# Last block's LayerNorm scales issued ahead of the ssm sums, its turns two products sooner, its sums in another order, one Square a product later

## The chip, the cores and the metric

The kernel runs on one core of a Trainium2 chip. Its engines are TensorE (PE in the profile; PEld is its weight load), VectorE (DVE), ScalarE (ACT), GpSimd (POOL) and SyncE (SP), which here only issues DMAs. The metric is the device time of one execution in microseconds (us). Before the change the median of three runs is 588.91 us (588.4 to 589.07).

## The reference

One transformer-like block on `x` of 2 x 2048 tokens by 512, with a condition vector per sequence, all in float32:

```python
emb = jnp.dot(silu(t), ada_w) + ada_b          # six rows of 512: shift, scale, gate for each half
norm = _ln(x) * (1.0 + scale_msa) + shift_msa
h = gelu(jnp.dot(norm, ssm_w1) + ssm_b1)       # exact gelu, 512 -> 512
x = x + gate_msa * (jnp.dot(h, ssm_w2) + ssm_b2)
norm2 = _ln(x) * (1.0 + scale_mlp) + shift_mlp
hf = gelu_tanh(jnp.dot(norm2, ff_w1) + ff_b1)  # 512 -> 1024
x = x + gate_mlp * (jnp.dot(hf, ff_w2) + ff_b2)
```

`_ln` takes mean and variance over the 512 features with eps 1e-6.

## The kernel before

**Tiles and blocks.** The 4096 tokens are cut into 8 blocks of 512, numbered 0 to 7. A block's `x` is a tile of 128 partitions by 4 rows by 512 features. Every matrix product is done by Strassen-Winograd schemes: seven products P1 to P7 of half-size operands in place of eight, with operands that are sums of quarters. The sums of the moving or the stationary operand are made by GpSimd or VectorE (`cut_sum`, line 348). The big ff product goes further, with 26 products (table `HK_P`) of registers that are sums of sixteenths (GpSimd, line 923, program `HK_B`).

**Stages.** For block i there are four products on TensorE: hA_i (first ssm product, line 475), oA_i (second, with the residual, line 475), hC_i (first ff product, 26 products in line 985, method `Second.products`), oC_i (second ff product, lines 778 and 824). For block 5, which the change speaks of, TensorE does in order hC_5, oA_6, hA_7, oC_5.

**LayerNorm.** Class `Norm`; n1[i] is the norm ahead of ssm, n2[i] the one ahead of ff. Its steps: statistics (`stats`, VectorE, lines 512 and 513; or on ScalarE, `sums_on_act`, line 524, and `squares_on_act`, line 535, with one tiny GpSimd operation `less`, line 540); `scales`, eight tiny GpSimd operations (lines 548 to 566) for 1/std and -mean/std; `normal(c)` for each of the four rows c on ScalarE (line 580); `turn(c)`, a 32 x 32 block transpose on VectorE (line 591) into the tile `blocks`; `move`, 16 DMAs of 64 KB issued by SP (line 600) that finish the transposition; `moved`, four ScalarE operations with scale and shift of the condition (line 623); `summed`, four sums for the Winograd operands (line 348). For n1[7] the four sums are made by VectorE into a tile `nS`: nS0 = q12 - q11, nS1 = q22 - nS0, q12 in place = q22 - q12 (`x<-x` in the profile), nS2 = q21 - nS1.

**Order.** Nothing is scheduled by a tool: each engine runs its instructions in the order in which the program issues them. `group` and `products` issue a product's matmuls, then what reads its PSUM bank (`after`), then the operations that were hooked to this product with `hook(hooks, places, ops)`, one place for each operation, the last place for all that are left. In `products` the places are the numbers 0 to 25. In a residual with the order `CARRIED` the products run as P1, P5, P6, P2, P7, P3, P4, but the places keep the names P1, P2, P6, P5, P7, P3, P4 by position: the place named P6 comes after the third product, P5 after the fourth, P7 after the fifth.

**PSUM.** In `products` there are six banks, two tiles for each of y, x and v. A bank is read by ScalarE for a destination's first term (line 999) or by VectorE for a further one (line 1002), and the next product into that bank waits for the reading; gelu is line 980. In a residual, P6, P7 and P4 (and P1) share bank y; VectorE reads a product into `x` in line 739, and P4 waits for the reading of P7.

**Where blocks differ.** In the loop from line 1278, `ahead` is true for i = 5 alone: there n1[7] is prepared in hC_5, and hA_7 follows oA_6 before oC_5. `unread_stats` is filled for i = 4 alone: the Squares of n1[6] are done by ScalarE inside hC_4 (line 1293).

Of the kernel before, what the change touches and what calls it, by code (L numbers as in the profile page):

```python
# [140 lines left out]
def kernel(  # L141
# [16 lines left out]
    nc = tc.nc  # L158
# [40 lines left out]
    def load_x(i, pieces=1):  # L199
        xs[i] = big_tile(f"x_{i}")  # L200
        for s in range(pieces):
            c = slice(s * C // pieces, (s + 1) * C // pieces)
            nc.sync.dma_start(out=xs[i][:, c, :], in_=x_blk[i][:, c, :])
# [209 lines left out]
    def leaves_of_weight(w_sb, s, engs):  # L413


        def views(w):
            v = w.rearrange("p (h k) (q e d) -> p h k q e d", h=2, e=2, d=P)
            return {f"{h + 1}{e + 1}": v[:, h, :, :, e, :] for h in range(2) for e in range(2)}

        lo, hi = w_sb[:, : w_sb.shape[1] // 2, :], w_sb[:, w_sb.shape[1] // 2 :, :]  # L420
        q23, t23 = views(hi), thirds(pair_t)
        o23 = second_operands(q23, t23)
        ops = {p: {n: v[:, :, j, :] for n, v in o23.items()} for j, p in enumerate(("P2", "P3"))}
        sums = {"P23": sums_of_second(q23, t23, engs["P23"])}
        for j, (p, w) in enumerate((("P4", s[:, 2]), ("P5", s[:, 0]), ("P7", lo[:, :, D // 2 :]))):
            q, t = {n: v[:, :, 0, :] for n, v in views(w).items()}, thirds(fw2_t[:, 2 + j])
            ops[p] = second_operands(q, t)
            sums[p] = sums_of_second(q, t, engs[p])
        return ops, sums
# [8 lines left out]
    def seed(name, row, part, leaf=False):  # L438


        b, cols = (("y", row[:, : D // 2]), ("v", row[:, D // 2 :]))[part]
        t = ps_g.tile([P, 2, HT], F32, tag=b, name=f"p{b}_{name}_{len(seeds.get((name, b), ()))}")
        seeds.setdefault((name, b), []).append(t)
        if part == 1 and leaf:
            nc.scalar.copy(t[:, 0, :P], cols[:, :P])
        else:
            nc.scalar.copy(t, cols.unsqueeze(1).to_broadcast([P, 2, HT]))
# [45 lines left out]
    def hook(hooks, places, ops):  # L493

        for n, op in enumerate(ops):
            hooks.setdefault(places[min(n, len(places) - 1)], []).append(op)
# [226 lines left out]
    def residual(name, i, hops, wops, kdim, hooks, last=False, order=ORDER):  # L723

        xt = xs[i]
        F = D // 2
        q = {
            "11": xt[:, 0:2, :F],
            "12": xt[:, 0:2, F:],
            "21": xt[:, 2:4, :F],  # L730
            "22": xt[:, 2:4, F:],
        }
        dest = {"P1": "11", "P2": "11", "P6": "12", "P5": "22", "P7": "22", "P3": "12", "P4": "21"}

        def after(p, ps, js):
            if p == "P1" and order is CARRIED:
                return
            d = q[dest[p]][:, js]
            nc.vector.tensor_tensor(d, ps[BANK[p]][:, js], d, ALU.add)  # L739
            if last and p in ("P7", "P4"):  # L740
                s = slice(2 + js.start, 2 + js.stop)
                f = slice(F, D) if p == "P7" else slice(0, F)
                nc.sync.dma_start(out=out_blk[i][:, s, f], in_=xt[:, s, f])

        parted = ("P1", "P6", "P7", "P4") if last else ()
        places = ORDER if order is CARRIED else None
        group(name, kdim, hops, lambda p, j, k: wops[p][:, k, :], after, hooks, parted, order, places)
# [306 lines left out]
    def run(ops):  # L1054
        for op in ops:
            op()
# [4 lines left out]
    n1 = {0: Norm(0, 1), 1: Norm(1, 1)}  # L1061
# [70 lines left out]
    gb, hA = {2: b2_bc}, {}  # L1132
# [12 lines left out]
    hooks = {}  # L1145
# [12 lines left out]
    hooks = {}  # L1158
# [26 lines left out]
    hooks = {}  # L1185
# [19 lines left out]
    hooks = {}  # L1205
# [14 lines left out]
    hooks = {}  # L1220
# [25 lines left out]
    hooks = {}  # L1246
# [10 lines left out]
    hooks = {}  # L1257
# [7 lines left out]
    hooks = {}  # L1265
# [11 lines left out]
    later, unread_stats = [], []  # L1277
    for i in range(1, NBLK):
        five = True
        nxt, nx2, last = i + 1 < NBLK, i + 2 < NBLK, i + 1 == NBLK  # L1280
        ahead, alone = i + 3 == NBLK, not nx2
        hC = Second(i)
        hooks = {}
        if i == 1:
            hook(hooks, range(0, 26), take(len(fa_sums)))
        if i == 1:
            engs = {"P23": nc.gpsimd, "P4": nc.gpsimd, "P5": nc.vector, "P7": nc.vector}
            leaf_wops, ops = leaves_of_weight(fw2_sb, fw2_s, engs)
            hook(hooks, (5, 7, 9, 11, 13, 14, 15, 16), ops["P23"] + ops["P4"])
            later = ops["P5"] + ops["P7"]  # L1290
            hook(hooks, (0,), [n1[i + 2].scales])
        elif unread_stats:
            hook(hooks, (1, 1, 3, 5, 7), unread_stats)
        if nx2:
            hook(hooks, (3,), [lambda: load_x(i + 1)])
            hook(hooks, (1, 2, 3, 4), hA[i + 1].summed(nc.gpsimd))
        elif nxt:
            hook(hooks, (1, 3), last_stats[2:])
            hook(hooks, (3,), [n2[i + 1].scales])
            hook(hooks, (15, 17, 19, 21), [lambda c=c: n2[i + 1].normal(c) for c in range(C)])  # L1300
            hook(hooks, (17, 19, 21, 23), [lambda c=c: n2[i + 1].turn(c) for c in range(C)])
            hook(hooks, (23,), [n2[i + 1].move])
        if nx2 and i > 1:
            hook(hooks, (7,) if unread_stats else (5,), [n1[i + 2].scales])
        if nx2:
            hook(hooks, (20, 24), [lambda p=p: seed(f"oA_{i + 1}", gb[2], p) for p in range(2)])
        else:
            hook(hooks, (20, 24), [lambda p=p: seed(f"oC_{i}", gb[5], p, five) for p in range(2)])
        if nx2:
            at = (12, 14, 16, 18) if i == 1 else (9, 11, 13, 15) if ahead else (15, 17, 19, 21)  # L1310
            hook(hooks, at, [lambda c=c: n1[i + 2].normal(c) for c in range(C)])
            hook(hooks, [n + 2 for n in at], [lambda c=c: n1[i + 2].turn(c) for c in range(C)])
            hook(hooks, (at[-1] + 2,), [n1[i + 2].move])
# [13 lines left out]
        hooks = {}  # L1327
# [12 lines left out]
        if nx2:  # L1340

            hook(hooks, ("P1",) if ahead else ("P7",), n1[i + 2].moved())
            if ahead:
                hook(hooks, ("P6", "P5", "P7"), n1[i + 2].summed(nc.vector, True))
            if i == 1:
                hook(hooks, ("P1", "P1", "P2", "P6"), later[:4])
            if fold:
                hook(hooks, ("P1", "P2", "P6", "P5"), fold[5:6] + fold[4:5] + later[:2])
            oC_seeds = [lambda p=p: seed(f"oC_{i}", gb[5], p, five) for p in range(2)]
            if not ahead:  # L1350
                hook(hooks, ("P2", "P6"), oC_seeds)
            n2[i + 1] = Norm(i + 1, 2)
            hook(hooks, ("P3", "P4"), n2[i + 1].stats())
            residual(f"oA_{i + 1}", i + 1, hA[i + 1], w2_ops, KD // 2, hooks, order=CARRIED)
            if ahead:
                hooks = {}
                hook(hooks, ("P2", "P6"), oC_seeds)
                hA[i + 2] = First(i + 2, n1[i + 2].ops, hooks, CARRIED, on_act=("P6", "P5"))
        else:
            for p in EARLY:  # L1360
                run(hooks.get(p, ()))
        leaf_fold, fold = (fold or i == 1) and later[2 if fold else 4 :], None

        hooks = {}
# [63 lines left out]
        hooks = {}  # L1428
# [7 lines left out]
        if i + 3 < NBLK:  # L1436
            st = n1[i + 3].sums_on_act() if refold5 else n1[i + 3].stats()
            unread_stats = n1[i + 3].squares_on_act() if refold5 else []
# [53 lines left out]
```

## Time and profile before

| | |
|---|---|
| median of three runs | 588.91 us (588.4 to 589.07) |
| the profiled execution | 589.1 us, span 587.3 us |
| granted TensorE clock | 0.999 |
| busy PE, PEld | 99%, 88% of the span |
| busy DVE, ACT, POOL | 71%, 45%, 73% |
| HBM read, written | 32.80 MB, 8.40 MB |

A line of a timeline has the start in us from the start of the span, the duration in us (of a merged group, from its first start to its last end), engine, line of the kernel, operation, written tile <- read tiles, partitions x elements, how many were merged, and in brackets how long the engine had been idle before it and what ended that. A line of waits has the waiting instruction, what it waited for, the total in us, how many times, and the longest. A line L348 or L923 is that of a helper; the tiles tell which step it is. hClo and hChi are the output of hC, hSC its sums, hSA the sums of hA.

### The profile page before, as it was taken

How to read it: one execution, taken by the hardware profiler on the slowest of the kernel's cores; microseconds unless marked ns; L12 is line 12 of the kernel's file. 1: busy time of each engine (PE TensorE's matmuls, PEld its weight loads, DVE VectorE, ACT ScalarE, POOL GpSimd, SP SyncE). 2: the span in 40 equal slices, each digit the busy share in tenths (PEclk: the TensorE clock that was granted, in tenths of full speed). 3: DMA queues.
4: the chain of work that ended last, by engine and by line, in shares of the span. 5: the costliest groups of instructions: out<-in, count | busy, mean ns of one | idle time of the engine just before them, and what ended most of it. 6: DMA issues, size and time to landing. Idle time of an engine off the chain costs nothing.

```text
span 587.3 us, 9483 instructions
## 1 busy us (share of the span) xinstructions
PE 579.2 (99%) x3303; PEld 516.4 (88%) x3303; DVE 415.9 (71%) x752; ACT 263.2 (45%) x479; POOL 428.4 (73%) x518
## 2 busy tenths in 40 slices
PE   8999999999999999999999999999999999999997
PEld 5888888888899888998889988998887998899896
DVE  4978888997867375676756858783747366787677
ACT  2234357405642554435732588235564431732420
POOL 1875359999997938969698899988587545369351
PEclk9999999999999999999999999999999999999999
DMA  8990322303206303361033711153030330031002
GB/s 316 395 392 9 91 68 81 104 37 107 59 15 187 119 1 81 111 203 71 6 87 83 276 73 31 42 140 145 4 73 0 104 113 1 1 73 71 2 1 71
DMA packets 25243, 56.49 MB, mean 96 GB/s; under 512 B 4672, under 2 KB 5740, under 8 KB 23532
## 3 DMA queue, kind: packets, MB, share of 16 engines
q1 hardware_dynamic: 21856, 51.67, 27.6%
q10 hardware_dynamic: 3340, 4.22, 2.9%
q8 instruction: 26, 0.43, 0.3%
q14 instruction: 21, 0.17, 0.1%
HBM read 32.80 MB, written 8.40 MB: 70 GB/s over the span
## 4 chain that ended last, share of the span: by engine, by line
PE 73%; POOL 11%; DVE 5%; DMA 5%; issue 3%; SPq 1%; ACT 1%; POOLq 0%; DVEq 0%
PE py_oA L475 7%; PE px_hC L985 7%; PE py_oC L778 7%; PE py_hA L475 7%; PE pl_oC_P_y L824 6%; PE py_hC L985 6%; PE pv_hC L985 6%; PE pl_oC_P_v L824 4%; PE pv_oA L475 4%; PE pv_hA L475 3%; PE py_oC L475 2%; PE py_hC L475 2%; DMA ada<-in_L_cond_ada_w_dram 2%; PE pl_oC_P_x L824 2%; POOL forms L923 2%
## 5 line engine op out<-in xcount | busy, mean ns | idle before, releaser
L348 POOL TENSOR_TENSOR hSC<-hClo,hChi 128x512 f32<-128x512 f32 (+1 forms) x16 | 19.2, 1205 | 40.8 <-ACT hChi L980 36.0
L623 ACT ACTIVATE nT<-nT,mod,mod 128x512 f32<-128x512 f32 x32 | 23.4, 802 | 55.6 <-DMA nT<-blocks 40.1
L512 DVE BATCH_NORM_STATS2 st<-x 128x6 f32<-128x512 f32 x60 | 40.7, 678 | 5.3 <-DMA x<-in_x_dram 5.0
L923 POOL TENSOR_TENSOR forms<-forms 128x256 f32<-128x256 f32 x56 | 41.8, 746 | 3.3
L985 PE MATMUL py_hC<-forms,fw 128*128 128x256 f32 x168 | 41.0, 380 | 0.1
L1002 DVE TENSOR_TENSOR hClo<-hClo,py_hC 128x512 f32<-128x512 f32 x42 | 28.6, 685 | 15.4 <-ACT hClo L999 9.4
L985 PEld LDWEIGHTS py_hC<-forms,fw 128*128 128x128 f32 x168 | 31.7, 190 | 4.9 <-DVE hClo L1002 0.5
L623 ACT ACTIVATE x<-x,mod,mod 128x512 f32<-128x512 f32 x24 | 17.6, 802 | 33.8 <-DMA x<-blocks 33.8
L591 DVE STREAM_TRANSPOSE blocks<-nT 128x512 f32<-128x512 f32 x32 | 22.2, 705 | 13.8 <-ACT nT L580 13.8
L923 POOL TENSOR_TENSOR forms<-nT,forms 128x256 f32<-128x256 f32 x42 | 30.6, 748 | 1.7 <-PE pl_oC_P_v L824 1.3
L1002 DVE TENSOR_TENSOR hChi<-hChi,pv_hC 128x512 f32<-128x512 f32 x35 | 23.3, 681 | 10.4 <-PE pv_hC L985 5.5
L923 POOL TENSOR_TENSOR forms<-nT 128x256 f32<-128x256 f32 x14 | 10.4, 740 | 27.6 <-ACT nT L623 20.7
L580 ACT ACTIVATE nT<-x,nmr,rstd 128x512 f32<-128x512 f32 x32 | 24.1, 806 | 13.2 <-POOL nmr L566 13.2
L985 PE MATMUL px_hC<-forms,fw 128*128 128x256 f32 x112 | 27.7, 380 | 0.5 <-ACT hClo L999 0.5
L980 ACT ACTIVATE hClo<-hClo,colsT 128x256 f32<-128x256 f32 x56 | 25.2, 498 | 4.2 <-DVE hClo L1002 4.0
L838 DVE TENSOR_TENSOR x<-pl_oC_P_y,x 128x256 f32<-128x256 f32 (+1 forms) x66 | 24.7, 375 | 3.1 <-PE pl_oC_P_y L824 1.5
L475 PE MATMUL py_oA<-w,hA 128*128 128x256 f32 x112 | 26.5, 379 | 0.0
L980 ACT ACTIVATE hChi<-hChi,colsT 128x256 f32<-128x256 f32 x56 | 25.1, 496 | 2.0 <-DVE hChi L1002 1.9
L739 DVE TENSOR_TENSOR x<-py_oA,x 128x512 f32<-128x512 f32 x26 | 17.9, 687 | 11.4 <-PE py_oA L475 10.8
L999 ACT ACTIVATE hChi<-py_hC 128x512 f32<-128x512 f32 x14 | 7.6, 593 | 40.9 <-POOL forms L923 21.0
L778 PE MATMUL py_oC<-fw_s,hSC 128*128 128x256 f32 x112 | 25.3, 380 | 0.0
L778 PE MATMUL py_oC<-fw,hClo 128*128 128x256 f32 x112 | 25.3, 379 | 0.0
(339 smaller groups left out, 1782.7 us busy)
## 6 DMA issues: line engine op xcount, KB each, us to landing
x<-in_x_dram SPq DMA_DIRECT2D x13, 1024.0 KB
out_dram<-x SPq DMA_DIRECT2D x14, 512.0 KB
ada<-in_L_cond_ada_w_dram SPq DMA_DIRECT2D x6, 1024.0 KB
x<-blocks SPq DMA_DIRECT2D x96, 64.0 KB
nT<-blocks SPq DMA_DIRECT2D x80, 64.0 KB
fw<-in_L_cond_ff_w_dram SPq DMA_DIRECT2D x2, 2048.0 KB
w<-in_L_cond_ssm_w_dram SPq DMA_DIRECT2D x3, 1024.0 KB
nT<-blocks ACTq DMA_DIRECT2D x48, 64.0 KB
```

Source lines behind the costliest of these rows:

```text
L475: nc.tensor.matmul(ps[b][j * apart][:, j, :], lhs(p, j, k), rhs(p, j, k), start=(fresh and j * (not apart) == 0 and k == 0), stop=(p in (" ...
L512: nc.vector.bn_stats(st, xs[self.i][:, c, :])
L580: nc.scalar.activation(t, x_c, AF.Identity, bias=self.nmr[:, c : c + 1], scale=self.rstd[:, c : c + 1])
L591: nc.vector.transpose(self.bl[:, :, :, c, :].rearrange("p m k q -> p k m q"), self.nT[:, c, :].rearrange("p (k m q) -> p k m q", k=KD, m=C),)
L623: nc.scalar.activation(dst, src, AF.Identity, bias=shift, scale=scale)
L778: yield lambda j=j, k=k: nc.tensor.matmul(ps[BANK[p]][:, j, :], hops(p, j, k), wops[p][:, k, :], start=False, stop=(k == kdim - 1), skip_g ...
L824: nc.tensor.matmul(t[:, n, :], hops.leaves[p][f][:, k, :], leaf_wops[p][f][:, k, :], start=room not in started, stop=(f in ("P2", "P3", "P ...
L838: nc.vector.tensor_tensor(d, src, d, ALU.add)
L923: eng.tensor_tensor(reg[d], reg[a], reg[b], ALU.add if f == "+" else ALU.subtract)
L980: nc.scalar.activation(h, h, AF.Gelu_apprx_tanh, bias=fb1T[:, m : m + 1])
L985: nc.tensor.matmul(ps[b][:, j, :], fa[ra][:, j * P : (j + 1) * P], fb[rb].rearrange("p a (c q) -> p c a q", q=Q), start=(fresh and j == 0) ...
L1002: nc.vector.tensor_tensor(dest(d), dest(d), ps[b], op)
```

## The change

Five hooks in the loop over the blocks move, the first for i = 4 and the others for i = 5. No instruction is added or taken away; TensorE's order is the same.

1. Block 4: the Square of row 0 of n1[6] is issued after product 2 and not after product 1.
2. Block 5: the four GpSimd sums of hA_6 are issued after products 3, 3, 4, 4 and not 1, 2, 3, 4.
3. Block 5: the scales of n1[7] are issued after product 1 and not 5. On GpSimd's queue they stand ahead of the sums of step 2 and no longer behind them.
4. Block 5: the normals of n1[7] are issued after products 7, 9, 11, 13 and not 9, 11, 13, 15; the turns, two products behind, after 9, 11, 13, 15; the move after 15 and not 17. On ScalarE the first normal comes ahead of the table load for gelu, on VectorE each turn comes two products sooner.
5. oA_6: the second sum of n1[7] is hooked to the third position and not the fourth, the third sum to the fourth and not the fifth. VectorE's order was reading of P6, nS0, reading of P2 (px), nS1, reading of P7 (py), x<-x, nS2; it becomes reading of P6, nS0, nS1, reading of P2, x<-x, reading of P7, nS2.

```diff
         elif unread_stats:
-            hook(hooks, (1, 1, 3, 5, 7), unread_stats)
+            hook(hooks, (1, 2, 3, 5, 7), unread_stats)
         if nx2:
             hook(hooks, (3,), [lambda: load_x(i + 1)])
-            hook(hooks, (1, 2, 3, 4), hA[i + 1].summed(nc.gpsimd))
+            hook(hooks, (3, 3, 4, 4) if ahead else (1, 2, 3, 4), hA[i + 1].summed(nc.gpsimd))
...
         if nx2 and i > 1:
-            hook(hooks, (7,) if unread_stats else (5,), [n1[i + 2].scales])
+            hook(hooks, (1,) if ahead else (7,) if unread_stats else (5,), [n1[i + 2].scales])
...
         if nx2:
-            at = (12, 14, 16, 18) if i == 1 else (9, 11, 13, 15) if ahead else (15, 17, 19, 21)
+            at = (12, 14, 16, 18) if i == 1 else (7, 9, 11, 13) if ahead else (15, 17, 19, 21)
             hook(hooks, at, [lambda c=c: n1[i + 2].normal(c) for c in range(C)])
             hook(hooks, [n + 2 for n in at], [lambda c=c: n1[i + 2].turn(c) for c in range(C)])
             hook(hooks, (at[-1] + 2,), [n1[i + 2].move])
...
             if ahead:
-                hook(hooks, ("P6", "P5", "P7"), n1[i + 2].summed(nc.vector, True))
+                hook(hooks, ("P6", "P6", "P5", "P7"), n1[i + 2].summed(nc.vector, True))
```

## The prediction

> **What bounds the kernel now.** I read the page's busy row first, then the list of waits kept to TensorE, then the timeline of the two places that the list led to.
>
> ```profile
> PE 579.2 (99%) x3303; PEld 516.4 (88%) x3303; DVE 415.9 (71%) x752; ACT 263.2 (45%) x479; POOL 428.4 (73%) x518
> PE py_oA L475 <- DVE x L739: 1.1, 1, 1.1
> PE px_hC L985 <- ACT hClo L999: 0.5, 1, 0.5
> ```
>
> TensorE is busy for 579.2 of 587.3 us, so an edit can only return what TensorE loses waiting. After the start (1.8 us of it) the list has just two waits, and both lie where the change works: in block 5's products, 408.6 to 432.15 us, and in the ssm product oA_6 behind them. A third, small one lies in block 4. The timeline shows what each is made of:
>
> ```profile
> 342.24 0.72 ACT L535 ACTIVATE unread<-x,less 128x512 f32<-128x512 f32 x1
> 342.95 0.59 ACT L999 ACTIVATE hChi<-px_hC 128x512 f32<-128x512 f32 x1
> 343.69 1.10 PE L985 MATMUL px_hC<-nT,fw_s 128*128 128x256 f32 x4
> ...
> 417.10 0.19 POOL L548 TENSOR_SCALAR ve<-mv 128x4 f32<-128x4 f32 x1
> 419.89 0.23 POOL L566 TENSOR_SCALAR nmr<-nmr 128x4 f32<-128x4 f32 x1
> 420.16 1.52 ACT L580 ACTIVATE x<-x,nmr,rstd 128x512 f32<-128x512 f32 x2 [1.63 <-POOL nmr L566]
> 421.58 0.57 ACT L999 ACTIVATE hClo<-px_hC 128x512 f32<-128x512 f32 x1
> 422.21 1.13 PE L985 MATMUL px_hC<-forms,fw 128*128 128x256 f32 x4 [0.49 <-ACT hClo L999]
> 424.28 2.00 PE L985 MATMUL py_hC<-forms,fw 128*128 128x256 f32 x8
> 427.26 10.02 SPq L600 DMA_DIRECT2D x<-blocks  x16
> ...
> 438.74 2.93 ACT L623 ACTIVATE x<-x,mod,mod 128x512 f32<-128x512 f32 x4 [4.03 <-DMA x<-blocks]
> 440.35 1.06 DVE L348 TENSOR_TENSOR nS<-x 128x512 f32<-128x512 f32 x1 [2.05 <-ACT x L623]
> 440.81 1.72 POOL L348 TENSOR_TENSOR hChi<-hChi 128x512 f32<-128x512 f32 x1
> 441.93 1.16 DVE L348 TENSOR_TENSOR nS<-x,nS 128x512 f32<-128x512 f32 x1
> 443.01 0.68 DVE L739 TENSOR_TENSOR x<-py_oA,x 128x512 f32<-128x512 f32 x1
> 443.74 1.99 PE L475 MATMUL py_oA<-w_s,hA 128*128 128x256 f32 x8 [1.06 <-DVE x L739]
> ```
>
> The reader should see three things. In block 4 a Square (L535) stands before the reading (L999) that frees a PSUM bank, and TensorE starts late at 343.69. In block 5 ACT sits idle until GpSimd's LN scales are done at 420.12, then two normals (L580) stand before the reading at 421.58, and TensorE starts product 15 late at 422.21. In oA_6 the tokens land at 438.74, DVE sums them between the readings, and the reading that frees bank y (L739, 443.01) comes late, so P4 starts at 443.74.
>
> In undisturbed stretches one product of four matmuls starts 0.8635 us after the one before. Block 5's 26 products should take 22.45 and take 23.55: **1.10 lost**, 0.76 at product 15 and 0.34 at product 17. oA_6's P4 should start six products of 1.727 after 432.15, at 442.51, and starts at 443.74, plus 0.10 for a first matmul whose weights were not preloaded: **1.33 lost**. Block 4 loses about **0.44** around 343.69. All that can be had here is 2.9 us, 0.5%.
>
> **The change part by part.**
>
> *Square, block 4 (gain b).* The bank's reading can follow the reading before it at 342.24 and end at 342.84, before product 5's weights are due near 343.1. That alone returns 0.38. But DVE's readings are late here as well, for another reason (its first waited for ACT until 341.96, the second of the fifth bank ends at 345.99), and product 8 needs the latter; its weights would be due at 345.75. So it waits until about 346.04, and b is 0.2; the ends are 0 (all given back) and 0.44. The Square itself moves into 342.7 to 343.6, where ACT was idle until 344.07.
>
> *Scales first on GpSimd.* Eight instructions, 417.10 to 420.12, go ahead of the four hSA sums, 411.94 to 417.02. Their input, DVE's statistics, is there at 409.45. They end at 415.1 and the sums at 420.1. TensorE first reads a sum at 433.67, so this costs nothing while 13 us of cover lasts; GpSimd was idle from 420.12 to 427.03 anyway. The sums could cost at most their delay of 3.1.
>
> *Normals and turns two products sooner (gain s).* ACT's order becomes: reading 415.71, normal, table load, two Gelu halves, two normals, reading. With start-to-start times from the same stretch (0.49 to a normal, 0.80 for it in full before the table load, 1.28, 0.42 and 0.40 for the halves, 0.72 and 0.70 for the normals) the reading starts at 420.55 and not at 421.58, and ends at 421.13. Product 15's weights are due at 421.34: no wait, by 0.2. Behind it lies a chain DVE, ACT, DVE to product 17, which took 2.13 from the reading's end (422.15) to 424.28; now it ends at 423.26 against a due time of 423.07, and only the unpreloaded matmul's 0.1 is lost. So s = 1.0; its ends are 0.5 (the reading 0.5 later) and 1.1. The later Gelus are read by GpSimd only at 427.03.
>
> [...] This trace shows 1.28 and no drain: the reading before the load ends at 416.31, the load runs from 416.32 and the Gelu starts at 417.62.
>
> *The move.* The last turn on DVE follows the chain above (d2 at 422.53, the reading of product 15 at 423.13, the turn at 423.73) and ends at 424.43, not 427.23. The 16 DMA issues on SP (10.02, about 0.63 each) start 0.03 behind it; SP had issued nothing since 407.5, so they pass nothing and delay nothing. Landing, 11.48 after the first issue, comes 2.80 sooner, and b on top: T = 435.74 for 438.74. TensorE is sooner by only s + b = 1.2.
>
> *The sums behind other readings.* DVE's order was nS, reading px, nS, reading py, x, nS. It becomes nS, nS, reading px, x, reading py, nS. One more sum (x<-x) now stands ahead of the reading that frees bank y for P4. What a sum costs there: 0.69 with GpSimd idle (58.87 us), but here four of four end 0.55 after the GpSimd sum that was running when they started (GpSimd's ended 440.85, 442.53, 444.21, 445.34; DVE's 441.40, 443.08, 444.76, 445.89), and GpSimd's next 512-element sum ends 1.13 after DVE's. The two engines alternate, one DVE sum every 1.68.
>
> In the new timing GpSimd's hSC sums, which start with TensorE's last readings, begin at 432.0 (433.20 less 1.2), and with the spacing of before the fifth runs from 437.04 to 438.31. The first nS is due 1.61 after T, at 437.35, in its middle: it ends at 438.86. The second then ends at 440.54 (1.68 later), x<-x at 442.22 (1.68 more), the reading py at 442.83, and P4's weights start at 442.88. P4 was at 443.74: **0.86 sooner**. TensorE's own due time for P4 is 441.31, so the stall grows from 1.33 to about 1.67. In short, the gain is s + b - 0.34. If DVE came first or GpSimd were out of the way, P4 would start at T + 6.32, 442.06: 1.68 sooner. If each time it just missed, T + 7.45, 443.19: 0.55 sooner. I take the middle case because the first nS falls 0.31 inside GpSimd's sum on one side and 0.96 on the other.
>
> Behind P4 nothing is late: the remaining nS ends at 443.9, and the list of waits has no TensorE entry to the end. GpSimd's sums for block 5's leaf products end by 458.6 and are read from 469 on; its forms for block 6 end 0.25 before those products begin but the last is used 20 us later.
>
> **Sum.** The profiled execution took 589.1 (span 587.3 and 1.8 around it); less 0.86 it is 588.2. The median of the three runs, 588.91, is 0.2 below that execution, so the forecast is 588.05, given as 588.0. This is 0.15% faster, and 0.2% (1.18 us) is about what a measurement of this kernel can tell from no change.
>
> **The rivals.**
>
> A. *The sums don't hold P4.* If the tokens land 0.31 us sooner against GpSimd than I work out, DVE's first sum starts before GpSimd's fifth and the chain gains 0.82; with all sums at 0.69 the stall all but goes, and the gain reaches 1.2 + 1.33 = 2.5. For: the turn's and GpSimd's starts are known to some 0.2 only. Against: four of four sums lost the race before. 586.4 to 587.3, chance 0.15.
>
> B. *ACT still holds the bank.* The reading waits behind normals as before, since the table load and Gelus now stand between them; s falls below 0.5. For: the margin at product 15 is 0.2. Against: ACT's idle 1.63 before the scales is removed in any case. With s + b from 0.7 down to 0 the end is s + b - 0.34 below 588.91: 588.5 to 589.3, chance 0.17.
>
> C. *Slower: the extra sum before the reading py decides.* At unchanged landing the new order puts P4 at 438.74 + 7.14 = 445.88, 2.14 later than now. The order pays only if the tokens land more than 2.14 sooner; I have 3.0. Without any earlier landing the end is at 591.1; it is slower by over 0.2% where the landing comes less than 0.96 sooner. For: the DMA issues take 10 us and the landing is the longest link, with nothing in the trace that shows it under another load. Against: SP issues at an even 0.63, and nothing else is on its queue. 589.4 to 591.1, chance 0.13.
>
> **How the numbers follow.** Forecast 0.55, by itself 587.6 to 588.6 (s + b from 0.65 to 1.65); A 0.15, B 0.17, C 0.13. Faster by over 0.2% (below 587.73): A and the forecast's lower edge, 0.25. Slower (above 590.09): 0.09 of C and 0.04 for what I don't see, 0.13. Within: 0.62. The range 586.9 to 589.4 leaves out C and the far half of A, 2 in 10.
>
> **What would show it.** Right: no ACT wait at product 15, reading L999 near 420.3, SP's first of 16 issues near 424.3, L623 near 435.7, and one TensorE wait on DVE x L739 of about 1.4 in oA_6, with DVE sums of 1.5 to 1.7 there. Block 4's product 5 starts at 343.3 and product 8 with a short wait. Wrong: the wait on L739 gone (A), L999 still after 421 (B), P4 later than 443.74 (C).

## The result, and the profile after

The changed kernel takes **588.20 us** (median of 22 runs, 588.11 to 588.30). The kernel before, run alternately with it, takes 589.09 (22 runs, 588.4 to 590.75). The medians differ by 0.89 us or 0.15%, less than the 0.2% that the prediction named as about what can be told. But the ratio of all these runs is 0.9983 with an interval of 0.9977 to 0.9990, which leaves out 1: the changed kernel is faster. The forecast was 588.0, a gain of 0.86. The profiled execution took 588.16 us with a span of 586.4, so the gain between the two profiled executions is 0.94.

The busy row of the page after:

```profile
PE 577.9 (99%) x3303; PEld 515.5 (88%) x3303; DVE 417.9 (71%) x752; ACT 263.1 (45%) x479; POOL 428.4 (73%) x518
```

DVE was busy for 415.9 us before and is now busy for 417.9, with the same 752 instructions. So some of them became slower. The list of waits of TensorE after is short:

```profile
PE py_oA L475 <- DVE x L739: 1.4, 1, 1.4
PE idle L1078 <- POOL ident masks.py:199: 1.3, 1, 1.3
PE rowsT L1087 <- DMA fw_t<-in_L_cond_ff_b_dram: 0.7, 1, 0.7
PE pada L275 <- DMA ada<-in_L_cond_ada_w_dram: 0.7, 2, 0.4
```

The last three belong to the start. ScalarE's entry (hClo, L999, 0.5) has gone. The wait for DVE in oA_6 has not: it grew from 1.1 to 1.4. The timeline after, in block 4, in block 5 and in oA_6, shows both:

```profile
342.26 0.60 ACT L999 ACTIVATE hChi<-px_hC 128x512 f32<-128x512 f32 x1
342.73 0.73 ACT L535 ACTIVATE unread<-x,less 128x512 f32<-128x512 f32 x1
343.39 1.03 PE L985 MATMUL px_hC<-nT,fw_s 128*128 128x256 f32 x4
...
415.51 0.60 ACT L999 ACTIVATE hClo<-px_hC 128x512 f32<-128x512 f32 x1 [2.13 <-PE px_hC L985]
416.01 0.81 ACT L580 ACTIVATE x<-x,nmr,rstd 128x512 f32<-128x512 f32 x1
416.83 1.28 ACT L980 ACT_TABLE_LOAD   x1
418.13 0.91 ACT L980 ACTIVATE hClo<-hClo,colsT 128x256 f32<-128x256 f32 x2
418.94 1.50 ACT L580 ACTIVATE x<-x,nmr,rstd 128x512 f32<-128x512 f32 x2
420.35 0.57 ACT L999 ACTIVATE hClo<-px_hC 128x512 f32<-128x512 f32 x1
421.36 1.03 PE L985 MATMUL px_hC<-forms,fw 128*128 128x256 f32 x4
423.08 1.96 PE L985 MATMUL py_hC<-forms,fw 128*128 128x256 f32 x8
424.24 10.01 SPq L600 DMA_DIRECT2D x<-blocks  x16
435.71 2.93 ACT L623 ACTIVATE x<-x,mod,mod 128x512 f32<-128x512 f32 x4 [2.24 <-DMA x<-blocks]
...
437.00 1.26 POOL L348 TENSOR_TENSOR forms<-hChi 128x512 f32<-128x512 f32 x1
437.32 1.50 DVE L348 TENSOR_TENSOR nS<-x 128x512 f32<-128x512 f32 x1 [0.26 <-ACT x L623]
438.35 1.60 POOL L348 TENSOR_TENSOR forms<-forms,hChi 128x512 f32<-128x512 f32 x1
438.93 1.57 DVE L348 TENSOR_TENSOR nS<-x,nS 128x512 f32<-128x512 f32 x1
441.02 1.16 DVE L348 TENSOR_TENSOR x<-x 128x512 f32<-128x512 f32 x1
442.10 0.68 DVE L739 TENSOR_TENSOR x<-py_oA,x 128x512 f32<-128x512 f32 x1
442.83 1.99 PE L475 MATMUL py_oA<-w_s,hA 128*128 128x256 f32 x8 [1.39 <-DVE x L739]
```

In block 4 the reading (L999) now stands ahead of the Square (L535), and product 5 starts 0.30 sooner. In block 5 one normal (L580) stands ahead of the table load and two between Gelu and reading, as the code now has it. The reading starts at 420.35, 1.23 sooner, and products 15 (421.36) and 17 (423.08) wait for nothing. The tokens land at 435.71, 3.03 sooner. Then the two sums of DVE take 1.50 and 1.57 us where an undisturbed sum takes 0.69, the third one, 1.16, now stands ahead of the reading that P4 needs, and P4 starts at 442.83. That is 0.91 sooner than before, and TensorE stays sooner by 0.91 to 0.93 from there to its last instruction.

A table of where TensorE stands against before gives the whole result:

| after | sooner by, us | what it says |
|---|---|---|
| product 8 of block 4 | 0.20 | step 1 kept this |
| product 17 of block 5 | 1.24 | steps 2 to 4 add 1.04 |
| P4 of oA_6 | 0.91 | the stall takes 0.33 back |

### The profile page after: what moved, and what is told of

The parts are those of the page before. It is cut to its first block, busy times and chain, and to the rows that moved or that the text cites. A ratio compares the mean times of both kernels' runs of the same rounds, so it can differ in the third digit from the quotient of the medians.

```text
span 586.4 us, 9484 instructions
## 1 busy us (share of the span) xinstructions
PE 577.9 (99%) x3303; PEld 515.5 (88%) x3303; DVE 417.9 (71%) x752; ACT 263.1 (45%) x479; POOL 428.4 (73%) x518
## 4 chain that ended last, share of the span: by engine, by line
PE 91%; DVE 3%; DMA 3%; issue 1%; ACT 0%; SPq 0%; DVEq 0%
PE px_hC L985 10%; PE py_hA L475 9%; PE py_oA L475 9%; PE py_hC L985 8%; PE py_oC L778 8%; PE pv_hC L985 8%; PE pl_oC_P_y L824 8%; PE pl_oC_P_v L824 5%; PE pv_hA L475 4%; PE pv_oA L475 4%; PE pl_oC_P_x L824 3%; DMA ada<-in_L_cond_ada_w_dram 2%; PE py_hC L475 2%; PE py_oC L475 2%; PE px_oA L475 2%; PE px_hA L475 2%
## 5 line engine op out<-in xcount | busy, mean ns | idle before, releaser
L923 POOL TENSOR_TENSOR forms<-forms 128x256 f32<-128x256 f32 x56 | 41.8, 746 | 3.3
L923 POOL TENSOR_TENSOR forms<-nT,forms 128x256 f32<-128x256 f32 x42 | 30.5, 748 | 1.8 <-PE pl_oC_P_v L824 1.3
L923 POOL TENSOR_TENSOR forms<-nT 128x256 f32<-128x256 f32 x14 | 10.4, 740 | 29.3 <-ACT nT L623 20.4
L580 ACT ACTIVATE nT<-x,nmr,rstd 128x512 f32<-128x512 f32 x32 | 24.1, 806 | 13.4 <-POOL nmr L566 13.4
L999 ACT ACTIVATE hChi<-py_hC 128x512 f32<-128x512 f32 x14 | 7.6, 593 | 41.1 <-PE py_hC L985 41.0
L739 DVE TENSOR_TENSOR x<-py_oA,x 128x512 f32<-128x512 f32 x26 | 17.8, 686 | 11.2 <-PE py_oA L475 10.6
L739 DVE TENSOR_TENSOR x<-pv_oA,x 128x512 f32<-128x512 f32 x16 | 11.0, 687 | 20.1 <-PE pv_oA L475 9.0
```

The lines of the kernel that those rows point to most:

```text
L580: nc.scalar.activation(t, x_c, AF.Identity, bias=self.nmr[:, c : c + 1], scale=self.rstd[:, c : c + 1])
L923: eng.tensor_tensor(reg[d], reg[a], reg[b], ALU.add if f == "+" else ALU.subtract)
```

## The experiments

The theory (T): steps 1 to 4 return 1.2 us, the earlier landing would also remove the stall at P4, and step 5, the new order of the sums, prevents that, because each DVE sum has to pass GpSimd's sums in turn. The rivals: the landing itself, or ScalarE, holds P4, whatever the order (R1); the sums cost only their own 0.69 us and GpSimd has no part in it (R2). Times of before are from runs on the same chip. P4's start and its wait are those of the traced execution, by its own clock (before: 443.74 and 1.1). In oA_6 the trace of steps 2 and 3 alone lies 0.49 us late and that of three sums 0.18 late against the changed kernel, and that of step 5 alone lies 0.2 early against before.

| kernel | median, us (range, runs) | before | ratio (interval) | P4 starts | its wait |
|---|---|---|---|---|---|
| after | 588.20 (588.11-588.30, 22) | 589.09 | 0.9983 (0.9977-0.9990) | 442.83 | 1.4 |
| all but step 5 | 586.52 (586.48-586.60, 5) | 588.94 | 0.9957 (0.9945-0.9969) | 441.26 | none |
| step 5 alone | 592.16 (591.31-592.25, 5) | 588.94 | 1.0049 (1.0037-1.0062) | 445.20 | 2.7 |
| step 1 alone | 588.91 (588.33-589.94, 11) | 588.94 | 0.9998 (0.9989-1.0007) | 443.60 | 1.0 |
| after, GpSimd quiet | 586.56 (586.46-587.32, 5) | 588.94 | 0.9961 (0.9949-0.9974) | 441.20 | none |
| steps 2 and 3 alone | 588.02 (587.91-588.46, 11) | 589.05 | 0.9982 (0.9973-0.9991) | 443.10 | 1.1 |
| step 4 alone | 592.42 (590.05-593.14, 4) | 589.05 | 1.0051 (1.0031-1.0070) | 447.68 | none |
| three sums first | 588.90 (588.80-593.33, 10) | 588.85 | 1.0014 (0.9997-1.0030) | 443.61 | 2.0 |
| four sums first | 592.23 (592.09-593.17, 4) | 589.05 | 1.0054 (1.0038-1.0069) | 445.11 | 3.6 |
| all but step 5, and row sums spread | 586.30 (586.19-586.33, 5) | 589.05 | 0.9953 (0.9941-0.9966) | 440.99 | none |

### All but step 5

The changed kernel with the old order of the sums:

```diff
-                hook(hooks, ("P6", "P6", "P5", "P7"), n1[i + 2].summed(nc.vector, True))
+                hook(hooks, ("P6", "P5", "P7"), n1[i + 2].summed(nc.vector, True))
```

> The whole change but for the order of block 7's sums in oA_6, which is that of before (nS0, reading px, nS1, reading py, x<-x, nS2). Theory (each VectorE sum ends 0.55 us after the GpSimd sum then running, so each sum ahead of reading py costs 1.68): the first sum ends at 438.8, reading py at 441.1, P4's weights start at 441.15 against a due time of 441.06; the wait of 1.4 is all but gone and the time is 586.6, 1.6 below the changed kernel. Rival 1 (the landing of the tokens holds P4, whatever the order): 588.2 as the changed kernel. Rival 2 (the new order of the sums is where the gain came from): 588.6 or more.

It took 586.52, 2.42 below before and 1.68 below the changed kernel. Its timeline in oA_6, VectorE and TensorE:

```profile
437.30 1.50 DVE L348 TENSOR_TENSOR nS<-x 128x512 f32<-128x512 f32 x1 [0.26 <-ACT x L623]
438.73 0.68 DVE L739 TENSOR_TENSOR x<-px_oA,x 128x512 f32<-128x512 f32 x1
439.33 1.15 DVE L348 TENSOR_TENSOR nS<-x,nS 128x512 f32<-128x512 f32 x1
440.40 0.68 DVE L739 TENSOR_TENSOR x<-py_oA,x 128x512 f32<-128x512 f32 x1
441.00 1.15 DVE L348 TENSOR_TENSOR x<-x 128x512 f32<-128x512 f32 x1
441.26 1.89 PE L475 MATMUL py_oA<-w_s,hA 128*128 128x256 f32 x8
```

The first sum is as late and as long as in the changed kernel (437.32, 1.50), but only two sums, not three, stand ahead of the reading that frees the bank. That reading runs at 440.40 in place of 442.10, and P4 starts with no wait at 441.26, when TensorE is done with the product before. R1 is out: ScalarE and the landing are the same here (the first sum starts within 0.02) and P4 doesn't wait.

### The changed kernel with GpSimd quiet

The hC sums of GpSimd that run beside DVE's are issued after oA_6, where those of the `sums35` group are; DVE keeps the new order.

```diff
-            hook(hooks, ("P5",), sums24)
+            hook(hooks, ("P5",), [] if ahead else sums24)
...
-            hook(hooks, ("P7",), sums7)
+            hook(hooks, ("P7",), [] if ahead else sums7)
...
-            hook(hooks, ("P1",), sums35)
+            hook(hooks, ("P1",), (sums24 + sums7 if ahead else []) + sums35)
```

> The changed kernel with its new order of sums, but GpSimd's eight leaf sums of hC_5 (forms, hChi, hClo) issued behind the LN scales of block 6, so that GpSimd is idle from 437.0 until about 448. Theory (the price of the sums is GpSimd's running sum): VectorE's four sums take 0.69 each, P4's weights start at 441.3 and the time is 586.7. Rival 1 (the sums take 1.2 to 1.5 whatever GpSimd does): 588.2. Rival 2 (the leaf sums are now late for oC_5, read from 467 on): a new TensorE wait in pl_oC and 588.2 or more.

It took 586.56, as much as without step 5. VectorE in oA_6 of this kernel, and P4:

```profile
437.23 0.69 DVE L348 TENSOR_TENSOR nS<-x 128x512 f32<-128x512 f32 x1 [0.25 <-ACT x L623]
438.58 0.69 DVE L348 TENSOR_TENSOR nS<-x,nS 128x512 f32<-128x512 f32 x1 [0.66 <-ACT x L623]
439.79 0.68 DVE L348 TENSOR_TENSOR x<-x 128x512 f32<-128x512 f32 x1
440.39 0.68 DVE L739 TENSOR_TENSOR x<-py_oA,x 128x512 f32<-128x512 f32 x1
...
441.13 1.59 PEld L475 LDWEIGHTS py_oA<-w_s,hA 128*128 128x128 f32 x8 [0.17 <-DVE x L739]
441.20 1.92 PE L475 MATMUL py_oA<-w_s,hA 128*128 128x256 f32 x8
```

The same three instructions that took 1.50, 1.57 and 1.16 take 0.69, 0.69 and 0.68. The second one even waits 0.66 for ScalarE. So the order by itself does no harm; the order beside a busy GpSimd does. R2 is out.

### Step 5 alone

```diff
-                hook(hooks, ("P6", "P5", "P7"), n1[i + 2].summed(nc.vector, True))
+                hook(hooks, ("P6", "P6", "P5", "P7"), n1[i + 2].summed(nc.vector, True))
```

This edit is made to the kernel before.

> The kernel before with the new order of the four sums alone. Theory: the tokens land at 438.74 as before, reading py comes one sum later (443.01 + 1.68), P4 starts at 445.4 for 443.74, the time is 590.8, 1.7 slower than before. Rival 1 (the order costs nothing, P4 waits for the landing): 589.1. Rival 2 (the order gains by itself): below 588.7.

It took 592.16, 3.22 above before, 1.4 more than expected. P4 starts at 445.20, later than before by 1.46. As the tokens land 0.19 sooner in this trace (438.55), the extra sum costs 1.65, and that was all that the expectation priced (1.68). The rest is lost behind the pause. Windows of this kernel (stretch, its length, busy time and instructions of PE, PEld, DVE, ACT and POOL, granted clock, DMA share, GB/s), one in the pause, one behind it, one later:

```profile
442.50:445.10 2.60, 0.00 (x0) 0.00 (x0) 2.60 (x5) 0.00 (x0) 2.60 (x2) 1.00 0.00 0
446.60:449.80 3.20, 3.20 (x10) 2.52 (x8) 2.47 (x6) 0.00 (x0) 1.10 (x2) 0.51 0.00 0
450.00:458.00 8.00, 8.00 (x38) 7.03 (x37) 1.32 (x5) 5.02 (x10) 6.21 (x12) 1.00 0.00 0
```

Behind the pause the granted clock is 0.51 and matmuls start 427 ns apart; later it is 1.00 and they start 216 apart. P4 and the product behind it take 1.68 us longer for it than they do in the kernel before.

### Step 1 alone

```diff
-            hook(hooks, (1, 1, 3, 5, 7), unread_stats)
+            hook(hooks, (1, 2, 3, 5, 7), unread_stats)
```

> The kernel before with the Square alone one product later. Theory: product 5 of block 4 starts 0.37 sooner, product 8 then waits for a VectorE reading and 0.2 is left: 588.9, and every later stall the same as before (the scales' and P4's are tied to TensorE or GpSimd alike). Rival 1 (all of block 4's loss of 0.44 returns): 588.65. Rival 2 (GpSimd's queue from block 4 on sets block 5's stall, so that the gain is eaten there): 589.1.

The time, 588.91 against 588.94, can't show 0.2 us. The trace can: product 5 starts at 343.42 (before 343.69), TensorE is sooner by 0.16 after product 8, and by 0.16 at the end; the waits behind it are unchanged.

### Steps 2 and 3 alone

```diff
-            hook(hooks, (1, 2, 3, 4), hA[i + 1].summed(nc.gpsimd))
+            hook(hooks, (3, 3, 4, 4) if ahead else (1, 2, 3, 4), hA[i + 1].summed(nc.gpsimd))
...
-            hook(hooks, (7,) if unread_stats else (5,), [n1[i + 2].scales])
+            hook(hooks, (1,) if ahead else (7,) if unread_stats else (5,), [n1[i + 2].scales])
```

> The kernel before with only the scales ahead of the ssm sums on GpSimd; normals, turns, move and sums as before. Theory: ScalarE no longer waits for the scales, the reading L999 starts at 420.0, products 15 and 17 don't wait, 1.1 is returned; the tokens land only 1.1 sooner (437.6), as much as TensorE moves, so P4 goes on waiting for about 1.4 and the time is 588.0. Rival 1 (the normals' place matters for products 15 and 17): a wait stays there, 588.5 to 589. Rival 2 (the earlier landing alone frees P4): 587 or less.

It took 588.02, 1.03 below before. Its profiled execution, the slowest of the 11 at 588.46, began 0.49 us late (a DMA wait at the start), so 0.49 is to be taken off its times:

```profile
420.50 0.60 ACT L999 ACTIVATE hClo<-px_hC 128x512 f32<-128x512 f32 x1
437.99 2.93 ACT L623 ACTIVATE x<-x,mod,mod 128x512 f32<-128x512 f32 x4 [3.91 <-DMA x<-blocks]
```

The reading L999 starts at 420.01 by the clock of the other traces, and products 15 and 17 don't wait. So the two moves on GpSimd alone return the whole of the 1.0; the earlier normals and turns add only the earlier landing. That landing here is 437.50, 1.24 sooner than before. The wait at P4 is unchanged at 1.1: TensorE and the tokens move together.

### Step 4 alone

```diff
-            at = (12, 14, 16, 18) if i == 1 else (9, 11, 13, 15) if ahead else (15, 17, 19, 21)
+            at = (12, 14, 16, 18) if i == 1 else (7, 9, 11, 13) if ahead else (15, 17, 19, 21)
```

> The kernel before with only the normals and turns two products sooner; the scales still end near 420.1. Theory: the first normal now holds ScalarE's queue, table load and gelu behind it, until 420.1; the reading L999 for product 15 ends near 425.1 for 422.15, product 15 waits 3.8, P4's wait of 1.3 goes; together 1.8 slower, 590.9, and if TensorE's clock is halved after so long a pause, some 1.7 more, 592.6. Rival (the turns sooner are worth it by themselves): 588.9 or less.

The time, 592.42, is near the second of the two values. The place of the loss is another than expected. Timeline of this kernel, ScalarE, VectorE and TensorE:

```profile
420.62 0.81 ACT L580 ACTIVATE x<-x,nmr,rstd 128x512 f32<-128x512 f32 x1 [4.30 <-POOL nmr L566]
421.46 0.71 DVE L591 STREAM_TRANSPOSE blocks<-x 128x512 f32<-128x512 f32 x1 [3.33 <-ACT x L580]
422.67 0.67 DVE L1002 TENSOR_TENSOR hClo<-hClo,py_hC 128x512 f32<-128x512 f32 x1
423.40 2.07 PE L985 MATMUL py_hC<-forms,fw 128*128 128x256 f32 x4 [2.53 <-DVE hClo L1002]
```

The scales still end late. ScalarE idles 4.30 us for them, the turn behind the normal idles DVE's queue for 3.33, and the reading that waits behind the turn frees bank y only at 423.3. TensorE stops for 2.5 us at product 14, through VectorE, where product 15, through ScalarE, had been expected. The products behind it run at half clock, by the window behind the pause:

```profile
423.50:430.00 6.50, 6.38 (x15) 4.62 (x16) 4.60 (x7) 4.73 (x9) 0.10 (x1) 0.51 0.00 0
```

TensorE is 2.71 late at product 14 and 5.16 late at 430; the stall at P4 then falls away, since the tokens are there 7.2 us before P4's place, and 3.84 is left. Steps 2 and 3 without step 4 are a gain, step 4 without them is a loss.

In oA_6 of this kernel the two engines meet the other way round:

```profile
443.38 0.68 DVE L348 TENSOR_TENSOR nS<-x 128x512 f32<-128x512 f32 x1
443.40 1.79 POOL L348 TENSOR_TENSOR forms<-hChi 128x512 f32<-128x512 f32 x1
```

DVE's first sum starts 0.02 us ahead of GpSimd's and takes 0.68; GpSimd's then takes 1.79, where the same one took 1.26 in the changed kernel. Here the one that starts first goes undisturbed and the other pays.

### Three and four sums first

Step 5 taken further, in the changed kernel: three, then four of DVE's sums ahead of the reading of P2.

```diff
-                hook(hooks, ("P6", "P6", "P5", "P7"), n1[i + 2].summed(nc.vector, True))
+                hook(hooks, ("P6", "P6", "P6", "P7"), n1[i + 2].summed(nc.vector, True))
```

and `("P6", "P6", "P6", "P6")` for four.

> The changed kernel with three of block 7's sums ahead of reading px and reading py, between the changed kernel (two ahead of px, a third ahead of py, pause 1.4, full clock after it) and the one with four (pause 3.6, half clock after it). Theory of the alternation: the third sum ends at 442.2 as in the changed kernel, the two readings follow, P4 starts at 443.4 for 442.83, pause 2.0. If the half clock needs a pause of more than 2.0 the time is 588.8; if a pause of 2.0 is already enough, about 1.7 more, 590.5.

> The changed kernel with all four sums of block 7 ahead of reading px and reading py. Theory: two more sums of 1.68 with GpSimd, less one that px had covered; P4 starts at 445.1 for 442.83, 2.3 later, 590.5; TensorE pauses for 3.6, and if the half clock seen with the new order alone (pause 2.7, 1.7 lost after it) comes from the pause, it comes here too and the time is 592.2. Rival (that loss belonged to something else in that kernel): 590.5.

With three, P4 starts at 443.61 (443.43 by the clock of the changed kernel, as this trace lies 0.18 later), with four at 445.11. The fourth sum costs 1.68, the alternation's one step. The third sum, which was ahead of P4 already, ends when it did (442.17 by that clock, 442.18 in the changed kernel). What its move costs, 0.6, is the reading of P2: it was done while this sum's turn had not come, and now it stands behind the sum. The list of waits gives pauses of 2.0 and 3.6. The windows behind them, first of three sums, then of four:

```profile
443.50:450.00 6.50, 6.39 (x30) 5.65 (x31) 5.56 (x12) 1.42 (x4) 3.69 (x6) 1.00 0.00 0
```

```profile
445.20:450.50 5.30, 5.30 (x13) 4.22 (x14) 2.87 (x7) 0.00 (x0) 1.42 (x3) 0.50 0.00 0
```

Behind 3.6 us TensorE runs at half clock and loses 2.7 more; behind 2.0, in this execution, it doesn't. Each execution's mean granted clock tells of the untraced ones. With three sums, six of ten took 588.80 to 588.96 at 0.998 to 1.0, while the three slowest, 590.51, 590.51 and 593.33, had 0.996, 0.997 and 0.993 (one of 589.57, at 0.999, fits neither). So, by their mean clocks, a pause of 2.0 is followed by half clock in some executions and not in others. Step 4 alone shows the same: 590.05 at 0.999, its three others 591.94 to 593.14 at 0.994 to 0.996. All 22 runs of the changed kernel, with its pause of 1.4, lie at 0.998 to 1.0.

### All but step 5, and the row sums spread

A delay of step 1's kind is left in block 4: ScalarE makes four row sums for n1[6] (L524) at the end of hA_5, and the first reading of block 4 stands behind the last of them. Here they are spread over hA_5:

```diff
-                hook(hooks, ("P6", "P6", "P5", "P7"), n1[i + 2].summed(nc.vector, True))
+                hook(hooks, ("P6", "P5", "P7"), n1[i + 2].summed(nc.vector, True))
...
-            hook(hooks, ("P7", "P7", "P4") if refold5 else ("P5", "P7", "P3", "P4"), st)
+            hook(hooks, ("P2", "P6", "P5", "P7") if refold5 else ("P5", "P7", "P3", "P4"), st)
```

> The changed kernel with the order of the sums of before, and the four row sums of n1[6] on ScalarE (L524) hooked one by one to places P2, P6, P5, P7 of hA_5 and not P7, P7, P4, P4. Theory (block 4's last 0.24 is lost because these four delay ScalarE's first readings in hC_4 to 341.3): the readings begin near 340.2, products 4 and 8 of block 4 don't wait, TensorE has no wait left after the start, the time is 586.3, 0.24 below the kernel with the old order alone. Rival (the row sums now delay hA_5's own readings): a new wait in hA_5 and 586.5 or more.

It took 586.30, 2.75 below before (0.47%) and the fastest of all. ScalarE in block 4 of this kernel:

```profile
340.01 1.08 ACT L999 ACTIVATE hChi<-py_hC 128x512 f32<-128x512 f32 x2
```

This reading started at 341.30 in the changed kernel. Behind the start TensorE has no wait left in the list, and from 54 us on no two of its matmuls start more than 0.3 us apart, so moving instructions in this way can return hardly anything more.

## Why the prediction was right

**The Square, b = 0.2.** Measured 0.20 in the changed kernel and 0.16 alone. Product 5 at 343.39 (343.3 said), and the weights of product 8 at 346.05 (346.04 said), held by the reading that DVE makes too late. The larger 0.44 was rightly not taken: DVE's first reading of block 4 waited for ScalarE, whose row sums stand in front, and when they were spread the remainder came.

**Normals and scales, s = 1.0.** Measured 1.04. The reading L999 was put at 420.55 without b, which is 420.35 with it, and came at 420.35. Product 17 starts on time, and its group, 1.96 us where an undisturbed one takes 1.89, loses 0.07 of the 0.1 left for it. One link was off: the scales were to end at 415.1 and end at 415.78, because GpSimd's forms ahead of them (L923) end 0.7 later in the changed kernel. That stayed hidden by 0.2 us, as ScalarE comes to the first normal only at 416.01. The prediction credited the 1.0 to scales, normals and turns together; the run of steps 2 and 3 alone shows that these two give it, and that step 4 adds 1.8 us of earlier landing. The table load, which now stands behind the first normal, costs this term no more than its own 1.28: the normal starts at 416.01 and takes 0.81, the load runs from 416.83 to 418.11, and Gelu starts at 418.13.

**The move.** The first DMA issue comes at 424.24 (424.3 said), the landing at 435.71 against T = 435.74.

**The sums, -0.34.** This is the term that decided, and it held to a few hundredths: GpSimd's fifth sum from 437.00 (437.04 said), the first nS until 438.82 (438.86), P4 at 442.83 (442.88), the stall 1.56 and 0.10 for the unpreloaded first matmul, 1.66 for 1.67. The two engines took turns as the prediction assumed. That the starts of both came within 0.04 is better than the prediction could claim, which knew them to some 0.2, and in part luck. The run with GpSimd quiet shows the cause that the prediction only inferred from four late sums. In the traces the sums take 0.69 alone and 1.50 or 1.57 beside GpSimd, and the readings L739, with one operand in PSUM, take 0.68 in both. What in the hardware makes the sums and GpSimd take turns, no run shows. The run with GpSimd quiet also shows a side price to be wrong: for GpSimd out of the way the prediction put P4 at T + 6.32, but there the weights of P4 start at 441.13, 5.51 after the landing at 435.62, and P4 starts on time. No run shows the 6.32 for a DVE that comes first.

**The rivals.** A (the sums don't hold P4) gave 586.4 to 587.3 and asked for a lucky 0.31 us against GpSimd. It isn't what the changed kernel does. But its mechanism exists: in step 4 alone DVE's first sum came 0.02 ahead and took 0.68. And its time is what two other kernels reach by removing one sum from the path or by moving GpSimd. B (ScalarE still holds the bank) is out by the waits. C (the extra sum decides, slower) is a true mechanism, without its condition: the landing came 3.03 sooner where 2.14 was needed. Where the landing isn't sooner, as in step 5 alone, it decides, and there its size was wrong. C puts P4 7.14 behind the landing, at 445.69 for this trace's 438.55. P4 came at 445.20, 0.5 sooner, because GpSimd's sums lay otherwise against that landing (the first nS took 1.05 and not 1.50). But the end came 1.1 above C's 591.1, because a pause was priced at its length. The pause of 2.7 us cost another 1.68 in the clock.

**What was missed** isn't in the sum but in its reading. The prediction had s + b = 1.2 and the stall of 1.33 in hand, and saw that step 5 adds one alternation of 1.68 ahead of P4. It named 2.9 as all that can be had and 2.5 as the gain of rival A, and didn't ask which step stands in its way. The runs answer that: step 1 returns 0.2, steps 2 and 3 return 1.03, step 4 the 1.2 that is left of 2.42 (by difference, as alone it is a loss), and step 5 takes 1.68 back.

## What to carry to other kernels

An earlier arrival of data is worth only what the order behind it lets through: here 3.0 us of earlier landing became a longer stall, because one more sum was put ahead of the reading that frees a PSUM bank. Before moving a VectorE sum like these ahead of a reading on the critical path, look at what GpSimd does in the same microseconds: beside GpSimd's sums one more of them cost a full turn of both engines here (1.68 us for these tiles), not its own 0.69. And a pause of TensorE can cost more than its length: the traced ones of 2.5 to 3.6 us here were followed by half clock, which lost another 1.7 to 2.7 us.

## What the runs showed of the hardware that was not expected

**Half clock after pauses of TensorE.** Pauses of TensorE of 2.5, 2.7 and 3.6 us were followed in the traced executions by a granted clock of 0.50 to 0.51, which cost 1.7 to 2.7 us; one of 2.0 brought it in some executions by their mean clock (0.993 to 0.997 in the three slowest of ten), one of 1.4 in none of 22 (0.998 to 1.0).

Windows on both sides show how long it lasts (length, busy time and instructions of the engines, granted clock, as above), first of step 5 alone, then of step 4 alone, then of four sums:

```profile
442.00:446.00 4.00, 1.28 (x7) 0.80 (x6) 4.00 (x6) 0.00 (x0) 3.92 (x4) 1.00 0.00 0
446.00:450.00 4.00, 4.00 (x12) 3.22 (x11) 3.24 (x7) 0.00 (x0) 1.71 (x3) 0.57 0.02 4
```

```profile
420.90:423.30 2.40, 0.00 (x0) 0.00 (x0) 1.84 (x3) 2.37 (x4) 0.00 (x0) 0.96 0.00 0
430.50:437.00 6.50, 6.50 (x32) 5.73 (x31) 3.78 (x6) 4.51 (x10) 4.41 (x4) 1.00 0.45 102
```

```profile
441.30:445.00 3.70, 0.17 (x1) 0.00 (x0) 3.70 (x5) 0.00 (x0) 3.62 (x4) 0.84 0.00 0
451.00:458.00 7.00, 7.00 (x34) 6.17 (x33) 0.96 (x4) 4.11 (x8) 5.22 (x11) 1.00 0.00 0
```

With those shown before, the half clock lasts about 3.4 us with step 5 alone (0.57 over 4 us, full on both sides), and about 6.8 us with step 4 alone (423.1 to 429.9) and with four sums (443.8 to 450.6). In the last two it begins 0.3 and 1.3 us before TensorE starts again. It doesn't follow the length of the pause: behind 2.7 us it is the shorter one, behind 2.5 and 3.6 the longer. What decides whether it comes, and for how long, is not shown; no run was made to find out. An estimate from these lengths: 3.4 us at half clock lose 1.7 of 590 (a mean of 0.997), 6.8 lose 3.4 (0.994). Most mean clocks of the slower untraced executions lie near one of the two.

**Spread of the runs.** The changed kernel's 22 runs lie within 0.19 us, those of before within 2.35. Why is left open; nothing was tried for it.
